# Layer 1 of a two-layer attention-convolution kernel: program order, transfers a column behind their source, GpSimd issuing v and results

## The chip, the cores and the metric

The kernel runs on one core of a Trainium2 chip, in float32. The metric is the device time of one execution in microseconds (us). The engines are named as in the profile: PE is TensorE (PEld its weight loads), DVE is VectorE, ACT is ScalarE, POOL is GpSimd, SP is SyncE. "SPq" and "ACTq" are the queues from which SP and ACT issue transfers (DMAs).

## The reference

Input x has shape (8, 56, 56, 384). Two layers follow each other, each with a group normalisation without parameters in front and a residual sum behind it:

```python
x = x + _L0_conv_ref(_gn(x), L0_conv_Wv, L0_conv_Wa, L0_conv_Wo)
x = x + _L1_conv_ref(_gn(x), W_attn, b_attn, W_v, b_v, W_proj, b_proj)

def _L1_conv_ref(x_map, W_attn, b_attn, W_v, b_v, W_proj, b_proj):
    k, heads = (3, 6)
    a = x_map @ W_attn + b_attn
    a = jax.nn.softmax(a.reshape(B, H * W, heads, k * k), axis=-1)
    v = x_map @ W_v + b_v
    vp = jnp.pad(v, ((0, 0), (1, 1), (1, 1), (0, 0)))
    patches = jnp.stack([vp[:, i:i + H, j:j + W, :] for i in range(k) for j in range(k)], axis=3)
    patches = patches.reshape(B, H * W, k * k, heads, hd)
    y = jnp.einsum('bpKhd,bphK->bphd', patches, a)
    return y.reshape(B, H, W, C) @ W_proj + b_proj
```

In layer 1 every pixel thus weighs the v vectors of its 3 x 3 neighbourhood, with nine softmax weights per head that come from its own logits. Layer 0 is of the same kind with 9 x 9 weights per pixel and a summing of overlapping windows; the change does not touch what it does.

## The kernel before

**Tiling.** The eight images are taken in four pairs. A column is one x position of both images of a pair: R = 112 rows. Seven columns (PX = 7) are a group, eight groups a pair, so layer 1 has NG = 32 groups and 224 columns. Its loop takes one column a step, `g, m = divmod(step, PX)`, and everything below is placed by m. Layer 1 occupies the end of the program, about from 2350 us of the profile's 3569.5 on.

**The stages of a group in layer 1.**

- `load(g)` brings the group's input `x1t` (1176 KB) from the memory table that layer 0 wrote. `normed` applies the group normalisation on ACT into `xns`, two buffers of eight columns.
- `attend(g, m)` projects a tile of 128 pixels into the accumulator `bank` (two in turn): 54 logits and 384 channels of v. DVE adds the biases, the logits go into the staging tile `lgt`, v into one of five tiles. `spread` writes v into the table `vtab1`, two transfers per tile, since a tile spans two columns. One column in eight has no tile.
- `regroup(g)` writes the staged logits to a table (`lgtab`) and reads them back by column (`at`), since tiles and columns don't align.
- `weigh(g)` is the softmax: maximum and difference on DVE, exponential on ACT, sum and reciprocal on DVE, and the product `at*den` on GpSimd.
- `move(g)` shifts the weights by rows on PE (`pw`), copies them on ACT into a band layout (`wz`), and writes them to one of three tables (`ztab`).
- `fetch(g, due)` issues the loads of the v patches (`vp`, two of 945 KB) and then of the band matrices (`z`, four of 258 KB), and puts the group's further work into a list of jobs with a due step: per image, two jobs of contractions z x vp on PE (accumulator `pc`, emptied by ACT into `yT`), then six output projections (`po`, to which DVE adds the bias and the residual into `x1t`), then transposes back (`turn`, PE then ACT into `ot`), and two result transfers per group. There are four z buffers, cut out of two large tiles, and four homes for `x1t`.

**What sets the order.** PE's instructions keep the program's order. ACT, DVE, GpSimd and the two transfer queues in layer 1 are ordered by a scheduler with its own estimate of times, which may move an instruction past others. `InOrder(engine)` is a wrapper, used so far in layer 0, that keeps an engine's instructions in the program's order. The jobs are run two per step, one at the step's start and one after `attend`; a group has fourteen, so jobs and steps balance.

**The places in the loop before:** `regroup(g - 1)` at m = 0, `weigh(g - 1)` at m = 2, `move(g - 1)` and `fetch(g - 1)` at m = 3 with the contractions due four columns later, `load(g + 1)` at m = 4, normalisation at m = 6 and m = 0:

```python
            if g and m == 2:
                weigh(g - 1)
            if g and m == 3:
                move(g - 1)
                while not clear_bands.done:
                    jobs.run(None, 1)
                fetch(g - 1, base + step + 4)
```

Of the kernel before, what the change touches and what calls it, by code (L numbers as in the profile page):

```python
# [15 lines left out]
def two_outlook_layers(  # L16
# [32 lines left out]
    nc = tc.nc  # L49
# [325 lines left out]

    def rows_to_patches(vp, table, px, r0, py, npy, sx):
        first = (px * (R + GAP) + GAP - MARGIN + r0) * sx * C
        nc.sync.dma_start(
            vp,
            bass.AP(  # L380
                table.tensor, table.offset + first, [[C, vp.shape[0]], [py * sx * C, npy], [1, C]]
            ),
        )
# [13 lines left out]
    def layer0(late, pools):  # L397
# [232 lines left out]
        def fetch_v(pair, px):  # L630

            vps[:] = [patch_tiles(f"0_{pair}_{px}", b) for b in range(IMG)]
            for b in range(IMG):
                rows_to_patches(vps[b], vtab0, px, b * H, PY0, NPY0, SX0)

# [147 lines left out]

    def layer1(pools, base, last_of_layer0, late_w):
        io = pools.enter_context(tc.tile_pool(name="io1", bufs=2))
        work = pools.enter_context(tc.tile_pool(name="work1", bufs=2))
        fixed = pools.enter_context(tc.tile_pool(name="fixed1", bufs=1))

        x1ts, lgs = {}, {}

        def load(g):
            pair, px = divmod(g, NPX)

            if g % 4 == 3:
                t = late_w.tile([P, NCH, T], F32, tag="xres", name=f"x1t_{g}")
            else:
                t = io.tile([P, NCH, T], F32, tag="x1t", name=f"x1t_{g}", bufs=3)
            nc.sync.dma_start(t, x1s[pair][px])
            x1ts[g] = t.rearrange("p i (m r) -> p i m r", m=PX)

        def normed(g, m0, m1):

            scale, bias = params1[g // NPX]
            first = g * PX
            cut = (first + m0) // SB * SB + SB
            for lo, hi in ((first + m0, min(cut, first + m1)), (cut, first + m1)):
                if lo >= hi:
                    continue
                to = xns[lo // SB % 2][:, :, lo % SB : lo % SB + hi - lo, :]
                for i in range(NCH):  # L810
                    for b in range(IMG):
                        rows = slice(b * H, (b + 1) * H)
                        nc.scalar.activation(  # L813
                            to[:, i, :, rows], x1ts[g][:, i, lo - first : hi - first, rows],
                            AF.Identity,
                            bias=bias[:, i, b : b + 1], scale=scale[:, i, b : b + 1],
                        )
# [4 lines left out]
        wc_t = fixed.tile([P, NCH, NC1], F32, name="wc1_t")  # L822
        nc.sync.dma_start(wc_t[:, :, :NA1], wa1.rearrange("(i p) n -> p i n", p=P))
        nc.sync.dma_start(wc_t[:, :, NA1:], wv1.rearrange("(i p) n -> p i n", p=P))

# [6 lines left out]
        wzs = [fixed.tile([R, NW + PX + 1], F32, name=f"wz1_{n}") for n in range(2)]  # L832

        NZ = 4
        half_z = NPY1 * PY1 * ROW1
        zs1 = [
            zs[n // 2].rearrange("p n e -> p (n e)")[: SX1 * SY1, n % 2 * half_z : (n % 2 + 1) * half_z]
            .rearrange("p (n e) -> p n e", n=NPY1)
            for n in range(NZ)
        ]  # L840

        def attend(g, m):

            col = g * PX + m
            if col % SB == 0:
                return
            tile_no = col % SB - 1
            tokens = xns[col // SB % 2].rearrange("p i m r -> p i (m r)")
            tokens = tokens[:, :, tile_no * P : (tile_no + 1) * P]
            pa = bank(P, 0, NC1, 2)  # L850
            project(pa, tokens, wc_t, 0, NC1)
            nc.vector.tensor_add(staged[-1][1][:, len(staged[-1][0])], pa[:, :NA1], ba_t)  # L852
            staged[-1][0].append(col // SB * NT + tile_no)
            v = work.tile([P, C], F32, tag="v", name=f"v_1_{col}", bufs=5)
            nc.vector.tensor_add(v, pa[:, NA1:], bv_t)
            for lo, n_col, row, n in parts_of(tile_no):
                c = col - col % SB + n_col
                spread(nc.scalar, vtab1, SX1, c % W, 1, row, v[lo : lo + n])

# [4 lines left out]

        def regroup(g):

            tiles, t = staged.pop(0)
            n = len(tiles)
            nc.scalar.dma_start(
                bass.AP(  # L870
                    lgtab.tensor, lgtab.offset + tiles[0] * P * NA1,
                    [[NA1, P], [P * NA1, n], [1, NA1]],
                ),
                t[:, :n],
            )
            lgs[g] = work.tile([R, PX, K2, HEADS1], F32, tag="at", name=f"at_1_{g}")
            nc.sync.dma_start(
                lgs[g].rearrange("r m k h -> r m (k h)"),
                bass.AP(
                    lgtab.tensor, lgtab.offset + g * T * NA1, [[NA1, R], [R * NA1, PX], [1, NA1]]  # L880
                ),
            )

        staged = []

        def weigh(g):

            at = lgs[g]
            heads_last = [R, PX, K2, HEADS1]
            mx = work.tile([R, PX, HEADS1], F32, tag="mx", name=f"mx1_{g}")  # L890
            nc.vector.tensor_reduce(mx, at.rearrange("r x k h -> r x h k"), AX.X, ALU.max)
            nc.vector.tensor_tensor(at, at, mx.unsqueeze(2).to_broadcast(heads_last), ALU.subtract)
            nc.scalar.activation(at, at, AF.Exp)
            den = work.tile([R, PX, HEADS1], F32, tag="den", name=f"den1_{g}")
            nc.vector.tensor_reduce(den, at.rearrange("r x k h -> r x h k"), AX.X, ALU.add)
            nc.vector.reciprocal(den, den)  # L896
            nc.gpsimd.tensor_tensor(at, at, den.unsqueeze(2).to_broadcast(heads_last), ALU.mult)  # L897

        def move(g):
# [14 lines left out]
            for kj in range(K):  # L914
                dst = wz[:, kj * K * ROW1 : kj * K * ROW1 + PX * step].rearrange("r (m e) -> r m e", e=step)
                dst = dst[:, :, : K * ROW1].rearrange("r m (e h o) -> r e m h o", e=K, h=HEADS1)
                for e in range(K):
                    nc.scalar.copy(dst[:, e, :, :, 0], pw[:, e, :, kj, :])  # L918
            table = ztab1[g % NTAB]
            nc.scalar.dma_start(  # L920
                bass.AP(
# [6 lines left out]
        def fetch(g, due):  # L928
# [5 lines left out]
            for b in range(IMG):  # L934
                rows_to_patches(vps[b], vtab1, px, b * H + MARGIN - 1, PY1, NPY1, SX1)
            for b in range(IMG):
                z, vp = zs1[(g * IMG + b) % NZ], vps[b]
                bands(
                    nc.sync, z, ztab1[g % NTAB], LINE1, SLOT1, ROW1, MARGIN - 1, GROUPS1,
                    b, PY1, NPY1,  # L940
                )

                def contract(t, b=b, z=z, vp=vp):
                    lo, hi = t * n_tile, min(NPY1, (t + 1) * n_tile)
                    pc = ps.tile([P, NCH, n_tile, PY1, PX], F32, tag="c", name=f"pc1_{g}_{b}_{t}", bufs=NC)
                    for py in range(lo, hi):
                        zp = z[:, py].rearrange("s (y h m) -> s y h m", y=PY1, h=HEADS1)
                        for h in range(HEADS1):
# [6 lines left out]
                            )  # L955
                    nc.scalar.copy(
                        yT[:, :, :, b, lo * PY1 : hi * PY1],
# [8 lines left out]
            def project_out(half, j):  # L966
# [4 lines left out]
                res = x1t[:, j, lo:hi].rearrange("p m r -> p (m r)")  # L971
                nc.vector.scalar_tensor_tensor(  # L972
                    res, po[:, :n], bo_t[:, j : j + 1], res, ALU.add, ALU.add
                )

            def turn(m):
# [6 lines left out]
                for i in range(NCH):  # L983
                    transpose(pt[:, i * P : (i + 1) * P], x1t[:, i, m, :], ident)
                nc.scalar.copy(fetch.ot[:, m - lo, :], pt)
                if m == hi - 1:
                    nc.sync.dma_start(
                        of[pair * R : (pair + 1) * R, px * PX + lo : px * PX + hi, :],
# [15 lines left out]
        stage(0)  # L1004
        for step in range(NG * PX + 4):
            g, m = divmod(step, PX)
            jobs.run(base + step, 1)
            if step == 0:
                last_of_layer0(base + step + 5)
            if step == 4:  # L1010
                for wz in wzs:
                    nc.gpsimd.memset(wz, 0.0)
            if g < NG:
                attend(g, m)
            if g and m == 0:
                regroup(g - 1)
                stage(g)
            if m == 4 and g + 1 < NG:
                load(g + 1)
            if m == 6 and g + 1 < NG:  # L1020
                normed(g + 1, 0, 3)
            if m == 0 and 0 < g < NG:
                normed(g, 3, PX)
            jobs.run(base + step, 1)

            if g and m == 2:
                weigh(g - 1)
            if g and m == 3:
                move(g - 1)
                while not clear_bands.done:  # L1030
                    jobs.run(None, 1)
                fetch(g - 1, base + step + 4)
        jobs.run(None, -1)
# [46 lines left out]
```

## Time and profile before

| | us |
|---|---|
| median of 3 executions | 3550.35 |
| lowest and highest | 3548.5, 3552.01 |
| the profiled execution | 3571.39 |
| its span in the trace | 3569.5 |

| queue | share of 16 DMA engines | MB |
|---|---|---|
| SP (q1) | 50.9% | 576.00 |
| ACT (q10) | 26.9% | 258.73 |

A row of the profile's groups reads: source line, engine, operation, output <- inputs, shape, count, then busy time, mean of one in ns, idle time of the engine before them and what ended it. A row of waits reads: who waited <- for what: us in total, times, longest. A source line can be that of a helper (L119 is the matmul, L122 the transpose, L317 the v write, L329 the z load, L378 the vp load), so the names of the tiles tell the stage. A low "granted clock" is the share of TensorE's full clock that it was given in a stretch.

### The profile page before, as it was taken

What the parts mean: (1) busy time and instruction counts of PE and PEld (TensorE: products, weight loads), DVE (VectorE), ACT (ScalarE), POOL (GpSimd) and SP (SyncE); (2) the same over time, 40 slices, a digit from 0 to 9 for tenths busy, and PEclk for the clock granted to TensorE, in tenths of its full rate; (3) what the DMA queues carried; (4) which work ended last, traced back from release to release, by engine and by line L of the source; (5) the groups of instructions that cost most, each with busy time, mean ns of one, the idle gap of its engine ahead of it and who ended that gap; (6) DMA issues with size and microseconds to landing.
All of it is one profiled execution on the core that took longest, in us unless ns stands there. A gap on an engine that the chain in (4) does not pass through costs nothing. (4 is left out here: it accounts for less than half of the span.)

```text
span 3569.5 us, 72083 instructions
## 1 busy us (share of the span) xinstructions
PE 3453.4 (97%) x29014; PEld 2365.3 (66%) x29014; DVE 1917.3 (54%) x4648; ACT 1165.0 (33%) x2727; POOL 984.5 (28%) x1409
## 2 busy tenths in 40 slices
PE   7899999999999999999999999989999999999998
PEld 5667767777777777777767767645565656556555
DVE  6666667667666676777666666532222222222322
ACT  4323233333333233333223323232333434334332
POOL 2543334344434434434434444310000000000000
PEclk8999999999999999999999999999999999999999
DMA  8999887688877778887667677677778787777876
GB/s 269 282 286 283 273 279 247 211 269 273 273 222 250 251 242 246 263 279 236 224 187 256 204 225 234 220 257 189 214 202 227 201 228 195 201 212 208 229 199 160
DMA packets 691452, 839.34 MB, mean 235 GB/s; under 512 B 302190, under 2 KB 595374, under 8 KB 687022
## 3 DMA queue, kind: packets, MB, share of 16 engines
q1 hardware_dynamic: 329614, 576.00, 50.9%
q10 hardware_dynamic: 361504, 258.73, 26.9%
q8 instruction: 228, 3.74, 0.5%
q14 instruction: 106, 0.87, 0.1%
HBM read 512.95 MB, written 321.66 MB: 234 GB/s over the span
## 5 line engine op out<-in xcount | busy, mean ns | idle before, releaser
L119 PE MATMUL bank<-wa_t,xn 128*112 128x288 f32 x4032 | 1087.3, 409 | 10.5 <-ACT v L562 6.8
L119 PEld LDWEIGHTS bank<-wa_t,xn 128*112 128x112 f32 x4032 | 693.8, 177 | 262.6 <-issue 34.6
L574 POOL TENSOR_TENSOR at<-at,den 112x972 f32<-112x972 f32 x224 | 504.6, 2253 | 1190.9 <-DVE den L573 1143.1
L119 PE MATMUL po<-yT,wo_t 128*128 128x448 f32 (+1 forms) x2304 | 820.6, 496 | 5.4 <-DVE x1t L685 4.8
L119 PEld LDWEIGHTS po<-yT,wo_t 128*128 128x128 f32 x2304 | 433.9, 191 | 294.7 <-issue 190.1
L119 PE MATMUL pc<-z,vp 121*32 121x49 f32 (+1 forms) x17664 | 491.9, 255 | 48.5 <-DMA z<-ztab 20.1
L119 PEld LDWEIGHTS pc<-z,vp 121*32 121x32 f32 (+1 forms) x17664 | 445.6, 132 | 125.5 <-issue 91.5
L119 PE MATMUL bank<-wc_t,xn 128*128 128x438 f32 x1176 | 495.6, 559 | 4.4 <-DMA wc_t<-in_wv 3.2
L550 DVE TENSOR_REDUCE mx<-bank 112x36 f32<-112x324 f32 x672 | 327.4, 487 | 307.3 <-PE bank L119 300.4
L119 PE MATMUL bank<-wv_t,xn 128*128 128x384 f32 x1176 | 419.2, 493 | 0.0
L897 POOL TENSOR_TENSOR at<-at,den 112x378 f32<-112x378 f32 x32 | 30.2, 943 | 1128.8 <-DVE den L896 925.1
L119 PEld LDWEIGHTS bank<-wc_t,xn 128*128 128x128 f32 x1176 | 220.1, 197 | 182.9 <-issue 172.1
L555 ACT ACTIVATE at<-at 112x972 f32<-112x972 f32 x224 | 227.0, 1014 | 349.4 <-DVE at L551 310.7
L551 DVE TENSOR_TENSOR at<-bank,mx 112x324 f32<-112x324 f32 x672 | 328.7, 489 | 21.1 <-DVE mx L550 0.5
L813 ACT ACTIVATE xn<-x1t,bias,scale 128x168 f32<-128x168 f32 (+4 forms) x498 | 213.7, 503 | 316.7 <-DMA x1t<-x 223.6
L119 PEld LDWEIGHTS bank<-wv_t,xn 128*128 128x128 f32 x1176 | 220.3, 191 | 140.0 <-issue 19.2
L972 DVE SCALAR_TENSOR_TENSOR x1t<-po,bo_t,x1t 128x448 f32<-128x448 f32 (+1 forms) x192 | 120.2, 626 | 324.1 <-PE po L119 324.1
L852 DVE TENSOR_TENSOR lgt<-bank,ba_t 128x54 f32<-128x54 f32 x196 | 41.4, 211 | 439.9 <-PE bank L119 439.9
L619 ACT COPY wt<-pw 112x120 f32<-112x120 f32 x224 | 58.1, 259 | 654.5 <-PE pw L119 573.6
L597 POOL TENSOR_TENSOR pre<-at,at 112x108 f32<-112x108 f32 (+1 forms) x440 | 237.1, 539 | 111.8 <-DVE wt L620 97.3
L567 DVE TENSOR_TENSOR d<-at 112x432 f32<-112x432 f32 x224 | 142.4, 636 | 204.3 <-ACT at L555 204.3
L664 ACT COPY yT<-pc 128x294 f32<-128x294 f32 x256 | 103.2, 407 | 373.6 <-PE pc L119 302.9
(92 smaller groups left out, 2806.8 us busy)
## 6 DMA issues: line engine op xcount, KB each, us to landing
z<-ztab SPq DMA_DIRECT2D x64, 2352.0 KB, 15.8
vp<-vtab SPq DMA_DIRECT2D x64, 1536.0 KB, 7.7
ztab<-wt ACTq DMA_DIRECT2D x336, 183.8 KB, 6.4
vp<-vtab SPq DMA_DIRECT2D x64, 945.0 KB, 9.7
xres<-xT SPq DMA_DIRECT2D x32, 1176.0 KB, 11.3
x1t<-x SPq DMA_DIRECT2D x32, 1176.0 KB, 9.5
xin<-xT ACTq DMA_DIRECT2D x54, 672.0 KB, 5.3
z<-ztab SPq DMA_DIRECT2D x128, 258.4 KB, 5.8
```

The costliest lines, as they stand in the source:

```text
L119: tc.keep_in_program_order(nc.tensor.matmul(*args, **kwargs))
L550: nc.vector.tensor_reduce(mx[:, pi, :], pl.rearrange("r q a -> r a q"), AX.X, ALU.max)
L551: nc.vector.tensor_tensor(at[:, pi], pl, mx[:, pi, :].unsqueeze(1).to_broadcast([R, K2, PH]), ALU.subtract)
L555: nc.scalar.activation(at, at, AF.Exp, scale=SCALE0)
L567: nc.vector.tensor_add(d4, at[:, :, 0:4], at[:, :, 4:8])
L574: nc.gpsimd.tensor_tensor(at, at, den.unsqueeze(2).to_broadcast([R, K, K2, PH]), ALU.mult)
L597: nc.gpsimd.tensor_tensor(dst, terms[0], terms[1], ALU.add)
L619: nc.scalar.copy(mid[:, 0 : E0 : E0 - 1, :], pw[:, 0 : E0 : E0 - 1, :])
L664: nc.scalar.copy(yT[:, :, :, b, rows_of], pc.rearrange("p i n y m -> p i m (n y)"))
L813: nc.scalar.activation(to[:, i, :, rows], x1ts[g][:, i, lo - first : hi - first, rows], AF.Identity, bias=bias[:, i, b : b + 1], scale=sca ...
L852: nc.vector.tensor_add(staged[-1][1][:, len(staged[-1][0])], pa[:, :NA1], ba_t)
L972: nc.vector.scalar_tensor_tensor(res, po[:, :n], bo_t[:, j : j + 1], res, ALU.add, ALU.add)
```

## The change

It is confined to layer 1 (`rows_to_patches` only gains the queue as an argument).

- ACT, DVE and SP are wrapped in `InOrder`: their instructions keep the program's order. In the loop, `weigh`, `share`, `move` and `normed` now stand ahead of the column's `attend`.
- The product `at*den` goes from GpSimd to DVE. The second half of the softmax becomes `share`.
- The v writes (before on ACT's queue) and the result writes (before on SP's) are issued by GpSimd, which has no arithmetic left there. The v write of a column is issued after the column's second job.
- Each transfer is issued a column or more after what it needs: the logits are written at m = 0 and read at m = 1; `weigh` is at m = 3, `share` at m = 4, `move` at m = 5; z and then vp are loaded at m = 0 of the group after, with the contractions due at m = 3; `x1t` of the next group is asked for at m = 1. A group's contractions begin three columns later than before. For the last group there are seven steps without projection, with places of their own.
- There are three z buffers, not four; the fourth half of the large tiles becomes a fifth home for `x1t`.

```diff
     def layer1(pools, base, last_of_layer0, late_w):
+        vector, scalar, sync = (InOrder(e) for e in (nc.vector, nc.scalar, nc.sync))
...
+        NZ = 3
+        half = NPY0 * PY0 * ROW0 // 2
+        halves = [z.rearrange("p n e -> p (n e)")[:, n * half : (n + 1) * half] for z in zs for n in range(2)]
...
-            if g % 4 == 3:
+            if g % 5 == 3:
                 t = late_w.tile([P, NCH, T], F32, tag="xres", name=f"x1t_{g}")
+            elif g % 5 == 4:
+                t = halves[3][:, : NCH * T].rearrange("p (i t) -> p i t", i=NCH)
             else:
                 t = io.tile([P, NCH, T], F32, tag="x1t", name=f"x1t_{g}", bufs=3)
-            nc.sync.dma_start(t, x1s[pair][px])
+            sync.dma_start(t, x1s[pair][px])
...
             v = work.tile([P, C], F32, tag="v", name=f"v_1_{col}", bufs=5)
-            nc.vector.tensor_add(v, pa[:, NA1:], bv_t)
-            for lo, n_col, row, n in parts_of(tile_no):
-                c = col - col % SB + n_col
-                spread(nc.scalar, vtab1, SX1, c % W, 1, row, v[lo : lo + n])
+            vector.tensor_add(v, pa[:, NA1:], bv_t)
+            return lambda: [
+                spread(nc.gpsimd, vtab1, SX1, (col - col % SB + n_col) % W, 1, row, v[lo : lo + n])
+                for lo, n_col, row, n in parts_of(tile_no)
+            ]
...
-            nc.scalar.activation(at, at, AF.Exp)
+            scalar.activation(at, at, AF.Exp)
+
+        def share(g):
+
+            at = lgs[g]
             den = work.tile([R, PX, HEADS1], F32, tag="den", name=f"den1_{g}")
-            nc.vector.tensor_reduce(den, at.rearrange("r x k h -> r x h k"), AX.X, ALU.add)
-            nc.vector.reciprocal(den, den)
-            nc.gpsimd.tensor_tensor(at, at, den.unsqueeze(2).to_broadcast(heads_last), ALU.mult)
+            vector.tensor_reduce(den, at.rearrange("r x k h -> r x h k"), AX.X, ALU.add)
+            vector.reciprocal(den, den)
+            vector.tensor_tensor(at, at, den.unsqueeze(2).to_broadcast(heads_last), ALU.mult)
...
             for b in range(IMG):
-                rows_to_patches(vps[b], vtab1, px, b * H + MARGIN - 1, PY1, NPY1, SX1)
+                bands(
+                    sync, zs1[(g * IMG + b) % NZ], ztab1[g % NTAB], LINE1, SLOT1, ROW1, MARGIN - 1,
+                    GROUPS1, b, PY1, NPY1,
+                )
+            for b in range(IMG):
+                rows_to_patches(sync, vps[b], vtab1, px, b * H + MARGIN - 1, PY1, NPY1, SX1)
...
                 if m == hi - 1:
-                    nc.sync.dma_start(
+                    nc.gpsimd.dma_start(
...
-        for step in range(NG * PX + 4):
+        for step in range((NG + 1) * PX):
             g, m = divmod(step, PX)
+
+
+            done, last = g - 1, g == NG
+            read, first, second, moved = (0, 2, 3, 4) if last else (1, 3, 4, 5)
             jobs.run(base + step, 1)
...
-            if g < NG:
-                attend(g, m)
-            if g and m == 0:
-                regroup(g - 1)
-                stage(g)
-            if m == 4 and g + 1 < NG:
-                load(g + 1)
+            if g and m == first:
+                weigh(done)
+            if g and m == second:
+                share(done)
+            if g and m == moved:
+                move(done)
             if m == 6 and g + 1 < NG:
                 normed(g + 1, 0, 3)
             if m == 0 and 0 < g < NG:
                 normed(g, 3, PX)
+            store = lambda: None
+            if g < NG:
+                store = attend(g, m)
             jobs.run(base + step, 1)
-
-            if g and m == 2:
-                weigh(g - 1)
-            if g and m == 3:
-                move(g - 1)
+            if g and m == 0:
+                keep_logits(done)
+                stage(g)
+            store()
+            if m == 1 and g + 1 < NG:
+                load(g + 1)
+            if g > 1 and m == 0:
                 while not clear_bands.done:
                     jobs.run(None, 1)
-                fetch(g - 1, base + step + 4)
+                fetch(done - 1, base + step + 3)
+            if g and m == read:
+                read_logits(done)
+            if last and m == 5:
+                fetch(done, base + step + 1)
```

The other lines of the diff replace `nc.vector`, `nc.scalar` and `nc.sync` by the wrapped engines, and split `regroup` into `keep_logits` (the write) and `read_logits`.

## The prediction, made before the changed kernel was run

> **What bounds the kernel now.** The page first. It names TensorE:
>
> ```profile
> PE 3453.4 (97%) x29014; PEld 2365.3 (66%) x29014; DVE 1917.3 (54%) x4648; ACT 1165.0 (33%) x2727; POOL 984.5 (28%) x1409
> PEclk8999999999999999999999999999999999999999
> ```
>
> A TensorE that is busy 97% leaves 116 us, and the question is how much of that lies in layer 1 and what a removed wait is worth there. In layer 1 the first matmul of the three-way shift (`pw`) comes once per group of seven columns, so two such starts bound a number of whole groups. The second is at 2417.68, the thirty-first at 3494.22: 29 groups. The table by windows, for these 29 groups, for the fastest of them, for one of the slowest, and for the end (columns: window and its length; busy time of PE, PEld, DVE, ACT, POOL; granted clock; DMA share; GB/s):
>
> ```profile
> 2417.68:3494.22 1076.54, 1034.93 (x7767) 645.08 (x7768) 301.21 (x645) 389.92 (x1168) 27.36 (x29) 0.97 0.78 208
> 2900.54:2934.78 34.24, 34.24 (x269) 21.54 (x268) 10.37 (x23) 12.89 (x37) 0.95 (x1) 1.00 0.90 234
> 2860.25:2900.54 40.29, 37.54 (x270) 23.45 (x268) 10.29 (x23) 12.56 (x37) 0.94 (x1) 0.92 0.75 209
> 3494.22:3569.50 75.28, 65.31 (x539) 42.38 (x537) 16.50 (x30) 18.61 (x57) 0.94 (x1) 0.96 0.67 164
> ```
>
> The same work takes 34.24 us with no idle moment at full clock, and 40.29 us with 2.75 us idle at clock 0.92. The mean is 1076.54/29 = 37.12. The fast group has six projections; the mean is 6.14 (1068 records, six each), and one more costs 2.2 us, so a clean mean group is 34.24 + 0.14 x 2.2 = 34.55. The 29 lose 1076.5 - 29 x 34.55 = 74.5 us. It splits cleanly: idle 1076.5 - 1034.9 = 41.6, and missing clock 0.03 x 1076.5 = 32.3. A wait costs its own length and three quarters again in clock. What TensorE waited for in these groups:
>
> ```profile
> PE pc L119 <- DMA z<-ztab: 15.3, 9, 3.0
> PE pc L119 <- issue: 13.2, 7, 3.3
> PE pw L119 <- POOL at L897: 8.6, 7, 1.5
> PE pc L119 <- ACT yT L956: 4.8, 5, 1.8
> PE pt L122 <- ACT ot L985: 0.6, 1, 0.6
> ```
>
> The "issue" waits stand before the same matmul as the z waits; in the chain of waits two of them (3436.18, 3474.74) follow a `ztab<-wz` and a `z<-ztab` directly, so I count them as z. ScalarE, which makes `wz` and empties the accumulators, is itself held:
>
> ```profile
> ACT xn L813 <- DMA x1t<-x: 223.6, 21, 13.2
> ACT ot L985 <- PE pc L119: 120.0, 35, 5.8
> ACT xn L813 <- DMA vtab<-v: 80.6, 7, 12.9
> ```
>
> One such hold in the timeline of ScalarE, in the slow group; its `ztab` write left at 2862.70, and SP's z loads only at 2876.54:
>
> ```profile
> 2862.70 0.32 ACTq L920 DMA_DIRECT2D ztab<-wz  x1
> 2866.28 0.78 ACTq L317 DMA_DIRECT2D vtab<-v  x2
> 2875.55 0.53 ACT L813 ACTIVATE xn<-x1t,bias,scale 128x168 f32<-128x168 f32 x1 [12.88 <-DMA vtab<-v]
> ```
>
> **What the Trainium skill says.** "DMA: Bandwidth & Descriptors", section "Issuing engines are not separate DMA queues": all issuers share the same 16 DMA engines, and another issuer saves only sequencer time. The trace agrees on traffic (78% share from two queues), so I expect no bandwidth from GpSimd, only a freed ScalarE. "TensorE: Matmul & The Clock Gate", section "What's actually happening": an idle window of about 3.4 us halves the clock. The trace shows the low clock (0.92 beside 2.75 us of idle) but after shorter waits too. "SBUF — State Buffer", section "SBUF: two separate sides": a transfer issued by GpSimd stalls while VectorE runs a two-port copy. No run here shows it, and VectorE's layer-1 list has no such SBUF copy.
>
> **The change part by part.** A column is 34.55/7 = 4.94 us; "m" is the column in the group.
>
> (1) The product `at*den` leaves GpSimd (0.94 us, 27.4/29) for VectorE. Nearest row: the subtract of the same shape, L892, 16.1/29 = 0.55 us. VectorE rises from 301 to 317 of 1076 us, hidden. `pw` now comes a column after the product, so its 8.6 us of waits go.
>
> (2) 355 v writes in 29 groups (12.24 each, the DMA view's rows summed) leave ScalarE's queue and two result writes per group leave SP's, for GpSimd. The v pairs take about 0.8 us of ACTq, so ScalarE's queue loses some 4.9 us per group. More: in the built program every SP or ACT transfer waits for the eighth before it, both engines counted together, so a v write of ScalarE can stand behind an x1t or result transfer of SP, with the normalisations and copies queued behind it. That is the 12.88 us above. After, ScalarE issues two transfers per group. GpSimd issues 14.24, each waiting for its own eighth; results queue there behind v writes, and v has five buffers (25 us). Price per GpSimd transfer: no row of before shows one. Below, the 0.4 us of an ACTq issue: 5.7 us per group. Above, the skill's fit ("DMA: Bandwidth & Descriptors", "Anatomy of one DMA — SWDGE (gpsimd) path"), 2.0 us plus bytes over 436 GB/s, strictly one after another: 14.24 x 2.0 + 2.71 MB/436 GB/s = 34.7 us, just the clean group. I take 1 us each, 14 us of 34.55, hidden, since eight may be in flight.
>
> (3) Order and lag. Before: move at m=3, contraction four columns later, 19.8 us. The chain by its rows: wz copies 1.0, ztab landing 12.7 (sharing with two vp loads issued beside it), four z issues 1.8, z landing 5.8: 21.3. It is 1.5 us short, which is the z wait (28.5/29 = 1.0). After: move at m=5, contraction five columns later, 24.7 us: slack 3.4 even at 12.7, and vp no longer goes out beside ztab. On SP z now precedes vp, so vp of image 0 lands behind 1.03 + 0.97 MB, 9.6 us at 208 GB/s; with ztab at 8 us, between a v write's 5 and 12.7, this ends about 4 us before it is needed; with 12.7 it is even. The vp loads wait for v writes of six columns back instead of two (25 such waits, 143.0 us on SP, go). x1t is asked for five columns ahead instead of two: the 223.6 us of ScalarE go, though they only partly reached TensorE. The logits' read, last on SP, stands behind z, vp and x1t, 4.1 MB or 20 us from m=6.9 (move at 5, then 1.0 + 0.3 + 8 us): it lands near m=3.9, where weigh stands at m=3. Behind weigh on VectorE stand the additions that empty a projection's bank, two banks deep, and share, whose product `pw` wants at m=5: mx, subtract, Exp, sum, reciprocal and product are 0.8 + 0.6 + 0.5 + 0.8 + 0.4 + 0.6 = 3.7 us or 0.75 columns, so TensorE notices only a landing after about m=4.3. Cost 0, bound 3 us per group.
>
> (4) ScalarE and VectorE in program order: ScalarE is 36% busy, VectorE 28%. Normalisation stands before the column's projection as its user needs it. The yT and ot waits (5.4) stay; I add 5 us of new ones, bounds -5 and +20.
>
> (5) Three z halves and five homes for x1t: each is free two columns before its load by the program's waits; nothing.
>
> (6) Start: group 0 contracts three columns later, with four projections (8.9 us) to cover a chain that took 14.8 (2385.48 to 2400.25); the wait grows from 4.2 to 5.9. With clock +2, bounds 0 and +6.
>
> (7) End: `pw` of the last group waited 3.2, z 0.6, and the clock was 0.96 over 75 us (3 us). One more column of work covers them: -5. The last result by GpSimd: +1, bounds 0 and +2.
>
> Sum: residual idle 10.4, with clock 10.4 x (1 + 32.3/42.5) = 18.3. Gain 74.5 - 18.3 = 56.2; start +2, end -4: -58. The profiled span is 3569.5 (that execution 3571.4), 19 us over the median 3550.35 of 3548.5 to 3552.0; an unprofiled run may hold slightly less wait, so I take -56: 3494.
>
> **The rivals.** A, the likeliest: as summed. Its own range: no residual and the start at its lower bound 3474; double residual 3512.
> B: the logits come late. If the read lands 0.7 us past that slack in every group, that returns 29 x 0.7 x 1.76 = 36 us: 3530. For it, mx already waits 76.9 us for this read and it now queues behind more; against, 2.6 us per group so far (76.9/29) and 0.4 columns of slack by my estimate.
> C, slower: GpSimd's issue becomes the bound. It decides from 34.55/14.24 = 2.43 us per transfer; at 2.61 the gain is gone; at 2.7 a group takes 38.4, 29 x 1.3 = +38: 3588. For it, no row prices the issue and in-order v writes would then run out of buffers and stop VectorE; against, that exceeds the skill's fixed cost with all of it in series.
> D: the DMA engines, not the order, are the limit (78%), and the waits come back elsewhere: 3550. Against: the fast group ran at a share of 0.90 and 234 GB/s with no idle.
>
> **How the numbers follow.** A 0.77, B 0.11, D 0.03, C 0.09. A and B are faster, D the same, C slower; a little of B's tail goes to slower: 0.87, 0.03, 0.10. 0.2% is 7 us, about what a measurement here can tell. The low end is A's; the high end takes in B and part of its tail: 3474 to 3540.
>
> **What would show it.** Right: `pw` starts 34.6 to 35.5 us apart, PE idle in 29 groups under 20 us, granted clock 0.99, no `pw` wait on the product, ScalarE's waits on x1t and vtab gone, ztab landing under 10 us. GpSimd transfers about 1 us apart at closest. Wrong: z waits still there, VectorE waiting over 5 us for the logits, or GpSimd's queue full with 2.4 us and more per transfer.

## The result, and the profile after

| | median, us | lowest to highest | ratio to before, 95% |
|---|---|---|---|
| before | 3551.18 (4 executions) | 3548.5 to 3559.18 | |
| after | 3516.78 (4 executions) | 3516.26 to 3521.11 | 0.9902 [0.9884, 0.9920] |

The changed kernel is faster by 34.4 us, 1.0%; the forecast was 56 us, 3494, with a range of 3474 to 3540 that holds 3516.78. The first part of the page, TensorE and GpSimd's v writes:

```profile
PE 3427.7 (98%) x29014; PEld 2353.0 (67%) x29014; DVE 1935.8 (55%) x4680; ACT 1173.3 (33%) x2727; POOL 1202.1 (34%) x1833
...
L317 POOL DMA_DIRECT2D vtab<-v x392 | 213.1, 547 | 825.3 <-DVE v L132 810.4
```

TensorE does the same 29014 matmuls in 26 us less busy time: that is clock, not work. A v write holds GpSimd 547 ns, and GpSimd sat idle most of the time, because v was not there yet. The table by windows of the changed kernel, for the 29 groups between the second and the thirty-first `pw`, for the end, and for the start; below it the start of the kernel before, from the same point:

```profile
2425.07:3429.57 1004.50, 1002.98 (x7764) 628.29 (x7762) 319.08 (x677) 402.95 (x1179) 224.83 (x415) 1.00 0.80 224
3429.57:3514.60 85.03, 69.59 (x577) 47.25 (x573) 15.71 (x27) 20.26 (x61) 5.96 (x12) 0.86 0.56 143
2328.60:2425.07 96.47, 80.09 (x701) 47.67 (x701) 30.38 (x82) 25.90 (x67) 24.37 (x32) 0.88 0.65 205
```

```profile
2328.60:2417.68 89.08, 75.90 (x730) 46.41 (x730) 29.42 (x79) 31.07 (x80) 9.92 (x4) 0.94 0.82 261
```

The groups fell from 1076.54 to 1004.50 us, 34.64 each, at full clock and with 1.5 us of idle time in all: the clean group of the prediction (34.55). Of these 72.0 us, 40.1 are idle time that went (41.6 to 1.5), and 32.0 are busy time of the same matmuls at a higher clock. The end went the other way, from 75.28 to 85.03 us at a clock of 0.86. The second `pw`, up to which the start reaches, came at 2425.07 instead of 2417.68. So the two spans differ by -72.04 + 7.39 + 9.75 = -54.9 us. The start and the end do not hold quite the same matmuls in both kernels (730 and 701 at the start, 539 and 577 at the end), so their sum is firmer than either alone. The waits of TensorE tell the same. Its longest entry for the groups (window 2417 to 3455), for the start (2330 to 2430) and for the end (3425 to 3515):

```profile
PE pc L119 <- ACT yT L132: 1.8, 5, 0.4
```

```profile
PE pc L119 <- DMA vp<-vtab: 10.4, 1, 10.4
```

```profile
PE pc L119 <- ACT yT L132: 5.2, 1, 5.2
```

Of the z waits, the `pw` waits and the "issue" waits of before, none is left between 2417 and 3455; the first contraction waits 10.4 us for vp (4.2 before, for z), and the last group's for ScalarE. What VectorE (in the 29 groups) and ScalarE (2417 to 3455) now wait for, and how long two transfers take from issue to landing (the last number of a row):

```profile
DVE mx L132 <- DMA at<-lgtab: 105.7, 29, 5.6
```

```profile
ACT ot L132 <- PE pt L122: 345.8, 66, 10.0
ACT at L132 <- DVE at L132: 97.3, 29, 5.3
```

```profile
ztab<-wz ACTq DMA_DIRECT2D x30, 496.1 KB, 4.4
...
lgtab<-lgt ACTq DMA_DIRECT2D x27, 162.0 KB, 11.7
```

ScalarE's waits for x1t and vtab (223.6 and 80.6 us) are gone but for one of 7.9 us; it now waits for TensorE's own transposes. `ztab` lands 4.4 us after its issue. VectorE's wait for the logits is hidden almost wholly in the 29 groups; what of it reaches TensorE, e6 shows below.

### The profile page after: what moved, and what is told of

It is laid out like the page before. It is cut to its first block, busy times and chain, and to the rows that moved or that the text cites. A ratio compares the mean times of both kernels' runs of the same rounds, so it can differ in the third digit from the quotient of the medians.

```text
span 3514.6 us, 72311 instructions
## 1 busy us (share of the span) xinstructions
PE 3427.7 (98%) x29014; PEld 2353.0 (67%) x29014; DVE 1935.8 (55%) x4680; ACT 1173.3 (33%) x2727; POOL 1202.1 (34%) x1833
## 5 line engine op out<-in xcount | busy, mean ns | idle before, releaser
L119 PE MATMUL pc<-z,vp 121*32 121x49 f32 (+1 forms) x17664 | 487.9, 254 | 25.3 <-DMA vp<-vtab 10.4
L317 POOL DMA_DIRECT2D vtab<-v x392 | 213.1, 547 | 825.3 <-DVE v L132 810.4
L119 PE MATMUL bank<-wc_t,xn 128*128 128x438 f32 x1176 | 478.8, 543 | 5.0 <-DMA wo_t<-in_wo 5.0
L132 DVE SCALAR_TENSOR_TENSOR x1t<-po,bo_t,x1t 128x448 f32<-128x448 f32 (+1 forms) x156 | 97.7, 626 | 248.9 <-PE po L119 248.9
L535 ACT ACTIVATE xn<-xin,bias,scale 128x224 f32<-128x224 f32 x336 | 172.9, 566 | 67.2 <-PE bank L119 36.0
## 6 DMA issues: line engine op xcount, KB each, us to landing
xres<-xT SPq DMA_DIRECT2D x32, 1176.0 KB, 10.1
```

Source lines behind the costliest of these rows:

```text
L119: tc.keep_in_program_order(nc.tensor.matmul(*args, **kwargs))
L132: return lambda *args, **kwargs: tc.keep_in_program_order(op(*args, **kwargs))
L317: queue.dma_start(bass.AP(table.tensor, table.offset + first, [[line, rows], [(R + GAP) * line - PX * C, n], [1, C]],), v.unsqueeze(1).to_ ...
L535: nc.scalar.activation(to[:, i, :, rows], xin[:, i, :, rows], AF.Identity, bias=bias[:, i, b : b + 1], scale=scale[:, i, b : b + 1],)
```

## The experiments

They ran on three chips, the kernel before beside each set: its medians there were 3580.39 us (e1 to e4), 3571.85 (e5 to e8) and 3565.77 (e9 to e12), so the ratios are to be compared, not the times of different sets. "Second pw", "groups" and "end" cut each profile's span in three, as above.

| run | median, us | ratio, 95% | second `pw` | 29 groups | end |
|---|---|---|---|---|---|
| first profile of before | 3550.35 | | 2417.68 | 1076.54 | 75.28 |
| first profile of after | 3516.78 | 0.9902 [0.9884, 0.9920] | 2425.07 | 1004.50 | 85.03 |
| e1 before | 3577.44 | 0.9994 [0.9983, 1.0005] | 2425.14 | 1071.14 | 74.5 |
| e2 order and places alone | 3723.47 | 1.0411 [1.0386, 1.0436] | 2437.41 | 1194.40 | 85.2 |
| e3 engines alone | 3624.47 | 1.0119 [1.0092, 1.0146] | 2428.72 | 1114.62 | 77.3 |
| e4 v by ScalarE | 3557.19 | 0.9940 [0.9921, 0.9960] | 2432.92 | 1036.15 | 83.5 |
| e5 after | 3531.43 | 0.9887 [0.9856, 0.9919] | 2431.43 | 1012.10 | 84.8 |
| e6 results by SP | 3630.47 | 1.0166 [1.0136, 1.0196] | 2432.52 | 1119.16 | 84.8 |
| e7 order by the scheduler | 3537.30 | 0.9906 [0.9878, 0.9934] | 2435.78 | 1027.51 | 78.9 |
| e8 ends repaired | 3522.39 | 0.9856 [0.9828, 0.9885] | 2428.00 | 1012.33 | 79.4 |
| e9 before | 3556.62 | 0.9979 [0.9967, 0.9990] | 2419.16 | 1080.75 | 74.0 |
| e10 after | 3526.05 | 0.9896 [0.9866, 0.9926] | 2429.43 | 1009.20 | 84.3 |
| e11 v in halves | 3530.90 | 0.9909 [0.9879, 0.9938] | 2428.40 | 1013.40 | 86.6 |
| e12 ends repaired | 3512.92 | 0.9862 [0.9828, 0.9895] | 2425.30 | 1009.98 | 75.7 |

### Two halves of the change, each alone

**e1**, the kernel before, unchanged.

> The kernel before, unchanged, to have a second profile of it. The profiled execution of before took 3571.4 us, its timed ones 3548.5 to 3559.2, while the changed kernel's profiled one lies among its timed ones. Theory 'spread': before's waits differ from execution to execution, and the first profile was a long one: the new profile lies within 3545 to 3560, with 20 to 30 us of PE idle in the 29 groups instead of 41.6. Rival 'the profiler lengthens the waits': the profile again lies near 3570, some 20 us over the timed runs. Timed median 3551 in both.

Measured 3577.44 us, equal to the kernel before within its interval. Neither expectation held: the median is not near 3551 but 27 us above the first three executions, so the level differs from one set of runs to the next, and the profiled execution (3572.73) lies below its median. The 29 groups:

```profile
2425.14:3496.28 1071.14, 1023.76 (x7768) 638.88 (x7768) 300.66 (x645) 388.92 (x1168) 27.37 (x29) 0.98 0.79 208
```

TensorE was idle for 47.4 us here, more than the 41.6 of the first profile, and yet the groups are 5.4 us shorter, since the clock was 0.98 and not 0.97.

**e2**, the order and the places of the change, with the engines of before: in the changed kernel,

```diff
-                spread(nc.gpsimd, vtab1, SX1, (col - col % SB + n_col) % W, 1, row, v[lo : lo + n])
+                spread(scalar, vtab1, SX1, (col - col % SB + n_col) % W, 1, row, v[lo : lo + n])
...
-            vector.tensor_tensor(at, at, den.unsqueeze(2).to_broadcast(heads_last), ALU.mult)
+            nc.gpsimd.tensor_tensor(at, at, den.unsqueeze(2).to_broadcast(heads_last), ALU.mult)
...
-                    nc.gpsimd.dma_start(
+                    sync.dma_start(
```

> The changed kernel with its program order and its places, but the v writes on ScalarE's queue, the results on SP's and the product on GpSimd again. Theory 'places': the later places and the order remove the z waits, the issuing engine matters little: 3517 to 3528. Rival 'issue': the gain came from a ScalarE freed of transfers; then ScalarE in program order is held by v writes that wait behind SP's transfers, and the time is 3540 to 3580.

Measured 3723.47 us, 4.1% slower than before, which none of the numbers above allowed for. TensorE's waits in its 29 groups:

```profile
PE pc L119 <- ACT yT L132: 107.4, 29, 7.4
PE pc L119 <- DMA vp<-vtab: 11.4, 10, 3.4
```

Once per group ScalarE, now in program order, comes late to empty an accumulator, for the instruction in front of it is held: in 27 of these 29 waits it is the exponential of the softmax, which waits for the logits (the timeline of e6 below shows one such wait). The loads of vp come late too. The product, on GpSimd but with the column's lag, costs only 0.2 us (one `pw` wait). e4 and e6 take this apart.

**e3**, the engines of the change, with the order and places of before (the three lines the other way round, in the kernel before).

> The kernel before with only the engines changed: v and results issued by GpSimd, the product on VectorE; scheduler's order and places as before. Theory 'places': the contraction still stands four columns behind the move, the chain of 21.3 us against 19.8 stays, only the waits on the product (8.6 us) go: 3538 to 3548. Rival 'issue': the chain gets shorter by itself, since ztab is written and z is asked for without holds: 3518 to 3530.

Measured 3624.47 us, 1.2% slower; this one missed too. Its waits in the 29 groups:

```profile
PE pw L119 <- DVE at L897: 44.3, 26, 4.3
PE pc L119 <- DMA z<-ztab: 11.0, 8, 2.8
```

The product on VectorE, without the column's lag, makes `pw` wait 44.3 us where it waited 8.6 before; ScalarE's wait for x1t stays (263.5 us, before 223.6). So the three moves together lose without the new places. How the v and result writes by GpSimd would do with the product left where it was is not shown: no run has that.

### Which issuer matters

**e4**, the changed kernel with the v writes by ScalarE, in program order (the first line of e2's diff alone).

> The changed kernel with the v writes alone back on ScalarE's queue, in program order. Theory 'places': ScalarE has room (36% busy) and most waits are on transfers long done: at most 10 us more, 3517 to 3527, with PE waits on yT of up to 10 us. Rival 'issue': a v write waits for the eighth transfer before it, SP's x1t (19 us to land) among them, and normalisations and copies stand behind it: 3535 to 3575, with ScalarE's waits named vtab or x1t back in the hundreds of us.

Measured 3557.19 us, a ratio of 0.9940, between the two expectations; the changed kernel has 0.9887 to 0.9902 in three comparisons, none of them beside e4. By the ratios v on ScalarE costs 14 to 19 us of the gain, by the groups (1036.15 us against 1004 to 1012) 24 to 32. The wait behind it is `pc <- yT`, 19.3 us, where "places" allowed 10; ScalarE's own waits for vtab stay under 10 us, where "issue" wanted hundreds.

**e5**, the changed kernel again, beside e6 to e8.

> The changed kernel unchanged, beside the kernel before on the same chip, since the executions of before lie at 3550 in one call and at 3580 in another. Theory 'before varies, after does not': TensorE sets the time of the changed kernel (1.5 us idle in 29 groups), so it comes out at 3510 to 3522 wherever it runs, and the gain is what before's waits are there, 35 us beside a before of 3551 and 60 to 68 beside one of 3580. Rival 'the chip is slower as a whole': after moves with before, 3540 to 3550, and the ratio stays 0.990.

Measured 3531.43 us, 40.4 below the kernel before on that chip. On this chip both kernels are slower, after by 15 us and before by 21. That is between the two expectations: the changed kernel varies from chip to chip as well, and the ratio (0.9887) stayed near 0.990. Its 29 groups:

```profile
2431.43:3443.53 1012.10, 1003.67 (x7764) 628.28 (x7762) 318.71 (x677) 402.19 (x1179) 224.82 (x415) 1.00 0.80 222
```

**e6**, the changed kernel with the result writes alone back on SP, in program order (the last line of e2's diff).

> The changed kernel with the result writes alone back on SP, in program order. In the run with order alone SP waited 598 us for ot. Theory 'results block SP': the writes of m=3 and m=6 stand ahead of the z, vp and logits' loads and hold them until ScalarE has copied ot; 3570 to 3680, with SP's wait on ot in the hundreds of us and PE waiting on yT and vp. Rival 'v writes did it': the loss of order alone came from the v writes on ScalarE's queue; then this run stays within 15 us of the changed kernel.

Measured 3630.47 us, 99 above e5; its groups are 107 longer. That results block SP is right, and of the pieces that were taken back one at a time it is the largest. It is not a share of the gain, though. SP's wait for the results' source in the 29 groups, in the kernel before, where the scheduler orders SP, and in e6:

```profile
SPq L987 <- ACT ot L985: 35.0, 17, 3.7
```

```profile
SPq L132 <- ACT ot L132: 308.1, 28, 14.2
```

So the 107 us are what program order would cost if the results stayed on SP at these places; a later place for them on SP was not tried. SP in the timeline of one group of e6:

```profile
2876.68 0.31 SPq L132 DMA_DIRECT2D at<-lgtab  x1
2886.60 10.12 SPq L132 DMA_DIRECT2D out<-ot  x2
2896.82 3.37 SPq L132 DMA_DIRECT2D z<-ztab  x4
```

The pair of results spans 10.1 us, since the second must wait until `ot` is transposed and copied, and the z loads stand behind it. But TensorE does not wait for z: 57.9 of its 69 us are for `yT`. The same group goes on:

```profile
PE pc L119 <- ACT yT L132: 57.9, 28, 4.1
```

```profile
2904.61 0.61 SPq L132 DMA_DIRECT2D at<-lgtab  x1
2920.95 0.83 DVE L132 TENSOR_REDUCE mx<-at 112x42 f32<-112x378 f32 x1 [7.40 <-DMA at<-lgtab]
2922.40 0.52 ACT L132 ACTIVATE at<-at 112x378 f32<-112x378 f32 x1 [7.10 <-DVE at L132]
2923.18 0.64 ACT L132 COPY yT<-pc 128x336 f32<-128x336 f32 x2
2923.68 2.19 PE L119 MATMUL pc<-z,vp 90*64 90x56 f32 x48 [2.21 <-ACT yT L132]
```

The logits' read goes out last, behind the results, z, vp and x1t, and VectorE starts on the logits 16.3 us later (11.5 in the mean of the 29 groups; 6.7 in the changed kernel). ScalarE's exponential waits for that, the copies to `yT` stand behind the exponential in program order, and TensorE waits for `yT`. In the timeline this is so in all 28 of these waits, and in all that the changed kernel has left in its 29 groups (4 waits in its first profile, 11 in e5, 6 in e10). It is the prediction's rival B, late logits, by a path that B did not name. No run puts the exponential behind the copies, or the logits' read further ahead, in every group. The windows row of e6:

```profile
2432.52:3551.68 1119.16, 1050.12 (x7763) 660.65 (x7761) 318.20 (x677) 400.38 (x1179) 193.72 (x358) 0.96 0.75 201
```

There are 69 us of idle time and 0.04 x 1119 = 45 us of missing clock (39 to 50, as the clock is given to two digits). Results on SP (107) and v on ScalarE (24 to 32) make up 131 to 139 of the 182 to 190 us by which e2's groups exceed those of the changed kernel. The rest lies with the product on GpSimd or with all three together; no run parts these.

**e7**, the changed kernel with ACT, DVE and SP left to the scheduler.

```diff
-        vector, scalar, sync = (InOrder(e) for e in (nc.vector, nc.scalar, nc.sync))
+        vector, scalar, sync = nc.vector, nc.scalar, nc.sync
```

> The changed kernel with ScalarE, VectorE and SP ordered by the scheduler instead of the program; places, engines and buffers as changed. Theory 'places and engines suffice': the chain has its five columns, 3515 to 3530. Rival 'order is needed': the scheduler moves the copies, the softmax or the loads to where its own times put them, and waits on z or on the product come back: 3545 to 3600.

Measured 3537.30 us, 5.9 above e5. The groups are 15.4 longer, the end 5.9 shorter. Neither expectation's number held, but z waits did not come back: TensorE's longest entry is 11.8 us for `yT`. The program's order, first in the change's description, is the smallest of the parts measured: given the places and the engines, the scheduler's order loses little. e3 and e7 together price the places: both have the new engines and the scheduler's order, and the groups take 1114.62 us with the old places and 1027.51 with the new places and buffers, 87 us less. No run has the new places with the old engines in the scheduler's order.

**e11**, every v write cut into two of 96 channels each.

```diff
                 for lo, n_col, row, n in parts_of(tile_no)
+                for c0, c1 in ((0, C // 2), (C // 2, C))
```

> Every write of v by GpSimd is cut into two halves of 96 columns: 24.5 v writes and 2 results per group instead of 12.2 and 2, the same bytes. Theory 'issue price 0.55 us, hidden': 26.5 x 0.55 = 14.6 us of a group of 34.6, so the time stays within 8 us of the changed kernel and POOL is busy about 215 us more (about 1420 us). Rival 'eight in flight': GpSimd's transfers wait for the eighth before them; at 26.5 per group each may take 8 x 34.6 / 26.5 = 10.4 us to land, and if they take longer (SP's take 12 to 19), GpSimd falls behind, v's five buffers run out, VectorE waits for v and the time rises by 40 us or more.

Measured 3530.90 us, 4.9 above e10, within what was expected of a hidden price. The group of v writes in its page:

```profile
L317 POOL DMA_DIRECT2D vtab<-v x784 | 421.5, 544 | 639.2 <-DVE v L132 590.9
```

Twice as many, each 544 ns, and GpSimd's idle time (639.2 us) is still mostly for v. POOL is busy 1411.7 us instead of 1204.6: 207 more, with 215 expected. GpSimd does stand behind earlier v writes now (14 waits, 17.1 us), without effect on TensorE. So GpSimd's issue (rival C) was far from being the bound.

### Where the missing part of the gain went

**e8**, the changed kernel with its ends repaired: the first group's logits are read by ScalarE a column earlier, the last group's go ahead of its second vp load, and the last results are issued by SP.

```diff
-            read, first, second, moved = (0, 2, 3, 4) if last else (1, 3, 4, 5)
+            read, first, second, moved = (0, 2, 3, 4) if last or g == 1 else (1, 3, 4, 5)
...
-            if g and m == read:
+            if g == 1 and m == 0:
+                read_logits(done, scalar)
+            if 1 < g < NG and m == read:
                 read_logits(done)
...
             for b in range(IMG):
+                if b and g == NG - 2:
+                    read_logits(NG - 1)
                 rows_to_patches(sync, vps[b], vtab1, px, b * H + MARGIN - 1, PY1, NPY1, SX1)
...
-                    nc.gpsimd.dma_start(
+                    (sync if g == NG - 1 else nc.gpsimd).dma_start(
```

> The changed kernel with its start and end mended: group 0's logits are read from ScalarE's queue a column earlier and its softmax and move stand a column earlier; the last group's logits are read ahead of the second vp load of the group before; the last group's two results go out from SP. If the waits at the edges cost what the profile shows (10.4 at the start, 5.2 at the end, each with low clock beside it, and some 3 us of the last write), this is 8 to 18 us below the changed kernel: 3499 to 3509. If the same chain only moves its wait elsewhere: within 4 us of it.

Measured 3522.39 us, 9.0 below e5, as the waits at the edges had it.

**e9 and e10**, both kernels unchanged on one chip.

> The kernel before once more, beside the changed kernel on the same chip, to see where the predicted 56 us became 34 to 40. Theory 'edges': in the 29 groups this execution is longer than the changed kernel's by 59 us or more (1071 against 1012 so far), and the changed kernel gives 15 to 20 us of it back at its two ends (start about 9.5 longer, end about 9.5 longer). Rival 'small waits': on one chip the 29 groups differ by only 35 to 45 us, since the 74.5 us lost in the profile of before were more than it loses in most executions, and the ends give nothing back.

> The changed kernel, unchanged, beside the one before. Both theories: 3515 to 3535 us, 40 +- 8 us under the kernel before. 'Edges': 29 groups in 1004 to 1013 us, start window 96.5, end window 85. 'Small waits': the same groups, but within 4 us of the kernel before at both ends together.

The windows of e9 for its 29 groups and its end, then those of e10:

```profile
2419.16:3499.91 1080.75, 1035.38 (x7768) 645.96 (x7769) 300.92 (x645) 390.68 (x1168) 27.38 (x29) 0.97 0.78 207
3499.91:3573.90 73.99, 65.22 (x539) 42.67 (x537) 16.49 (x30) 18.65 (x57) 0.94 (x1) 0.96 0.66 167
```

```profile
2429.43:3438.63 1009.20, 1004.88 (x7764) 629.13 (x7762) 319.01 (x677) 402.92 (x1179) 225.71 (x415) 1.00 0.79 223
3438.63:3522.90 84.27, 68.65 (x577) 46.87 (x573) 15.72 (x27) 20.32 (x61) 5.98 (x12) 0.88 0.58 144
```

The groups differ by 71.6 us and the start and end return 10.3 each, a little more than "edges" had it; "small waits" (35 to 45 us in the groups) is wrong of these two profiles. Yet it holds a grain: the spans differ by 51.0, the medians by 39.7 from all executions of before there (30.6 from e9's own). The profiled execution of e9 took 3575.81 us, the highest of its twenty, whose median is 3556.62; in the very first profile it was 3571.39 beside 3550.35. For the changed kernel they agree: 3516.74 beside 3516.78, 3525.01 beside 3526.05. The unprofiled executions of before therefore lose some 20 us less than two of its three profiles show. In e1 the profiled execution was not above its median, so it need not be so; in e6 and e7 it was the slowest of its four, in e2 and e4 the fastest. Whether the profiling slows a kernel that waits for transfers, or these executions came from the upper edge by chance, stays open.

The record has each execution's span and mean granted clock, and they say what varies. Of e9's twenty the fastest spans 3546.6 us at a clock of 0.989, the slowest, the profiled one, 3573.9 at 0.982. As an estimate, (1 - clock) x span is 39 and 64 us: 25 of the 27 us between them are clock. Whether the waits differed as well no unprofiled run shows.

**e12**, the kernel of e8 again.

> The changed kernel with its two ends repaired (first logits read by ScalarE a column earlier, last logits read ahead of the last vp load, last results by SP), again, beside the changed kernel on one chip. Theory 'edges': 9 us under the changed kernel (start 3 shorter, end 5.5 shorter, 29 groups within 3 us). Rival 'drift': the 9 us of the first comparison lay in the groups or between executions, and it is within 3 us of the changed kernel.

Measured 3512.92 us, 13.1 below e10. In the spans 11.9: start 4.1, end 8.6 shorter, groups 0.8 longer. "Edges" holds and "drift" falls; this version has the lowest median in both comparisons (in the second its range, 3501.84 to 3520.84, overlaps that of the changed kernel).

## Why the prediction was right, and where its sum was not

The direction and the mechanism were right; the time was 23 us too low. It lies 5 us outside the likeliest case's own range (A, 3474 to 3512) and inside the stated one only because that was widened for rival B, whose loss did not occur; that part is luck. By its steps:

- **The bound and the clean group.** Right. 34.55 us was the forecast for a group without waits; 34.64 (after), 34.90 (e5) and 34.80 (e10) were measured. Clock 1.00 where 0.99 was named. The split of the loss was less clean than it looked: a clock of 0.97 to two digits stands for 27 to 38 us, not for 32.3, and "three quarters again in clock" is no fixed price (last section).
- **(1) The product.** Right: no `pw` wait in the groups. It was the column's lag, not VectorE, that did it: VectorE without the lag waits 44.3 us (e3), GpSimd with it 0.2 (e2).
- **(2) GpSimd's price.** 1 us was taken between 0.4 and 2.4; it is 0.55, so 14.24 x 0.55 = 7.8 us per group. The sum does not change, as the forecast had it hidden. I named a freed ScalarE as the gain of this part; once the engines keep program order, freeing SP of the results is worth three to four and a half times as much in the groups (e6 against e4). I had costed SP's side at nothing.
- **(3) Order and lag.** Right in kind: z waits gone. `ztab` landed in 4.4 us, where 8 were taken. Logits were the nearest to the bound, as said: in one group the product ends at 2908.6 and `pw` begins at 2909.80.
- **(4) New waits of in-order engines.** A residual idle time of 10.4 us was taken; 1.5 (after), 8.4 (e5) and 4.3 (e10) were measured, with a clock of 1.00 and not the 7.9 us of missing clock that the sum set beside them. The waits left are those for `yT` behind the exponential. So the groups gained 72.0 and 71.6 us where the sum had 56.2.
- **(6) The start failed.** The sum had +2, with a wait of 5.9. It kept the old chain of 14.8 us and set it against four projections. But part (3) had put vp behind z on SP, and vp then closes the chain. In the timeline `pw` starts at 2391.98, z is issued at 2398.28, vp at 2400.39, and the contraction starts at 2412.09: 20.1 us, of which the projections cover 9.0, and TensorE waits 10.4. The bound of +6 did not hold either: the start is 7.4 us longer (10.3 in e9 and e10), at a clock of 0.88 where it was 0.94.
- **(7) The end failed in sign.** The sum had -4. SP at the end of the changed kernel:

```profile
3437.76 1.07 SPq L132 DMA_DIRECT2D vp<-vtab  x2
3447.47 0.31 SPq L132 DMA_DIRECT2D at<-lgtab  x1
```

The last logits' read is issued only at 3447.47: SP waits 8.6 us for the logits' write, which ScalarE issued at 3437.03, to land. VectorE idles 6.2 us for it at 3454.23, ScalarE with its exponential stands in order ahead of `yT`, and TensorE waits 5.2 us at 3456.96. I had counted the added column as cover, and not asked what the in-order engines hold up when the read is late. The last result by GpSimd was taken at +1; from the end of its issue to the end of the span it takes 8.5 us (3506.1 to 3514.6), with SP 4.8 (3564.7 to 3569.5, and again in e8 and e12): +3.7. Start and end together return 17 to 21 us, where the sum had -2.
- **From the span to the median: the step that failed most.** The sum against its own span was -58, and the spans differ by -54.9 (-51.0 in e9 and e10), because an excess of 16 us in the groups and a shortfall of 19 at the ends nearly cancel; that it came so close is luck. I then took 2 us off for "an unprofiled run may hold slightly less wait". It was about 20: the profiled execution lay 21 us above the median. What varies from one execution of before to the next is mostly its clock, as e9's twenty show. They spread over 27 us, the changed kernel's sets of four over 12 at most.
- **The rivals.** B: the logits do come later (mx waits 105.7 us in the 29 groups, 76.9 before). They reach TensorE by ScalarE's exponential and `yT`, not by `pw`, and cost 1.5 to 8.4 us of idle time where B had 36 us. C: refuted by 0.55 us and e11. D: the DMA share rose only from 0.78 to 0.80 while the waits went. The Trainium skill ("DMA: Bandwidth & Descriptors", "Issuing engines are not separate DMA queues") says that another issuer saves sequencer time alone. The runs agree on the traffic, but e6 shows what that can hide: with the same bytes, the choice of the queue in which two results stand was worth 107 us in 1119, since in program order a transfer that waits for its source held all loads behind it.

## What to carry to other kernels

When a kernel is bound by short waits, look at what stands in order behind each waiting transfer: in a queue that keeps program order, results that wait for a last computation don't belong ahead of the loads which feed the next stage. Look also at what stands ahead of each copy that empties an accumulator; here it was an exponential that waited for a load. Lag with program order (e2) and new issuers (e3) each made this kernel slower alone; together they made it faster. Count the ends of a pipelined stretch by themselves, with the new order of every queue, and don't subtract a profiled execution's waits from the median of others: ask first whether that execution lies above them.

## What the runs showed of the hardware

- A wait of TensorE can cost more than its length, but not at a fixed price. In the kernel before a wait of 1.35 us (to 2453.53) was followed by 3.41 us at half clock:

```profile
2454.10:2457.51 3.41, 3.41 (x9) 1.77 (x8) 0.00 (x0) 1.54 (x11) 0.00 (x0) 0.50 0.63 148
```

Over 29 groups 69.0 us idle stand beside a clock of 0.96 (e6), 66.7 beside 0.96 (e3), 45.4 beside 0.97 (e9), 47.4 beside 0.98 (e1), and 8.4 us, in waits of up to 1.5 us, beside 1.00 (e5). What decides whether a short wait lowers the clock, these runs do not show.
- GpSimd issued a v write in 0.55 us, whole or half (547 ns in the mean of the changed kernel, 544 in e11).
- From the end of the last result's issue to the end of the span it took 8.5 us by GpSimd (after, e5, e10) and 4.8 us by SP (before, e8, e12).
- The same kernel differed on one chip by 0.2% in two sets of twenty and more executions (e9: 0.9979 [0.9967, 0.9990]); an interval from one chip is not quite the whole uncertainty, and a difference of 0.2 to 0.3% is not to be read from one comparison.
